# A state-space block on one Trainium2 core: channel chunks in interleaved pairs, tiles in pieces of two chunks, column-grouped sums

## The chip, the cores and the metric

The kernel runs on one core of one Trainium2 chip. A core has five instruction queues that run side by side: TensorE (PE in the profile: matmuls, results into PSUM), VectorE (DVE), ScalarE (ACT), GpSimd (POOL) and SyncE (SP, which here issues nearly all DMA transfers). The metric is the time of one execution on the device in microseconds, the median of several runs. The profile shows one more execution, with every instruction's start and end.

## What is computed

The input x is 8 images of 384 channels by 1024 positions, all in float32. Each image goes through a Mamba-like block and then (all but three of them) through a binarised MLP:

```python
t = layernorm(x over channels)                          # twice normed in the reference
xm, z = split(t @ in_proj_w.T)                          # 768 channels each
xc = silu(conv_w[0]*xm[l-2] + conv_w[1]*xm[l-1] + conv_w[2]*xm[l] + conv_b)
dt, Bm, Cm = split(xc @ x_proj_w.T, [24, 24 + 16])
dt = softplus(dt @ dt_proj_w.T + dt_proj_b)
for n in range(16):                                     # states, for each of 768 channels
    h[n][l] = exp(dt[l] * A[n]) * h[n][l-1] + dt[l] * xc[l] * Bm[l, n]
    y[l] += h[n][l] * Cm[l, n]
y = (y + xc * D) * silu(z)
x = x + gelu((y @ out_proj_w.T) @ mlp_w1.T + b1) @ mlp_w2.T + b2
```

The second layer works on the result: `x + bitlinear(gelu(bitlinear(layernorm(x), W1, b1)), W2, b2)`. A bitlinear takes the sign of W less its mean, in five groups of output rows, multiplies, and scales and clips the result by the largest absolute value over one image. Its groups cover five of the eight images; for the others this layer adds nothing.

## The kernel before

**Units of work.** Channels lie on the 128 partitions, positions along the free dimension, in two halves of T = 512. For image b:

- `s1(b)`, the front: norm, `in_proj` (p_in, p_z), the convolution, SiLU, `x_proj` (p_dbc), the rows of B and C (p_bc), `dt_proj` (p_dt), softplus, and the product dt times xc. The results xc, z, dt, dtx (dt times xc) and the B and C rows go to DRAM.
- `s2(b)`, the state space: `scan` takes 64 channels at a time (12 units an image). A tile has 32 channels times 4 states on its partitions, and 1024 positions. There are 8 tiles a unit: two groups of channels times four quads of states. For each tile ScalarE makes da = exp(A dt), GpSimd multiplies dtx by the row of B (L886, the B product) into u, VectorE runs the recurrence (L890), and the product with C follows, on GpSimd (L904) or VectorE (L907), as `on_pool` (L866) says. TensorE adds up the states through the small matrix `fold` into py (L842), 32 output rows a matmul, so that four matmuls share the array. Then y is gated with z and goes to DRAM as yg. Images 0 and 7 go through in halves, with the state carried between them; there one tile holds two groups of 32 channels by 512 positions.
- `s3(b)`: out_proj (p_out), the MLP (p_h, p_o), and the residual.
- `ffn(b)` for the first five images: the second layer. `binarise` (once for each of W1 and W2) adds up W with a matrix of ones (p_sums, L1018), takes the means (L1030), and writes the signs to DRAM.

**Order.** `write_down` lists all operations with what each reads and writes. `Plan.run` then sets the order on each queue ahead of time: it simulates the five queues with the costs given to `add`, and takes at each step an operation whose inputs and buffers are ready, by priority (sums of py first, then the scan of the current image, then fronts of the next two images, then `s3` and `ffn`). On the chip each queue runs in that fixed order and waits on semaphores. Where the plan leaves TensorE without work for more than 0.7 us it puts in stand-in matmuls (`spare`, L412), whose result nobody reads.

**Buffers.** Each tile belongs to a ring of a fixed number of buffers (L369 to L386), and a buffer comes free when its last reader is done. Those that the change touches: `front` (2 of six chunks: xc, dt, z), `dt_r` and `dtx_r` (3 each of 1024), `u` (9 tiles of 1024), `da` (2, in PSUM), `yg` (1 of six chunks), `hid` (2 of six chunks), `res` (2), `small` (7), and `sq` (1, the squares of the norm). A chunk is 128 channels by 512 positions.

**Helpers.** `load` (L462), `store` (L469) and `weights` (L484) issue one DMA on SP; `matmuls` (L489) issues n matmuls that add up in one PSUM bank; `act` (L506) is one ScalarE function; `affine` (L516) goes to ScalarE or, if it is free sooner, to VectorE or GpSimd.

Of the kernel before, what the change touches and what calls it, by code (L numbers as in the profile page):

```python
# [42 lines left out]
HK = KH // 2  # L43
T = 512
# [49 lines left out]

def c_pool(n):
    return 0.18 + n * 0.00214
# [33 lines left out]
class Piece:  # L130
# [8 lines left out]

    def __getitem__(self, part):  # L140
        return self, part

# [209 lines left out]
class Layer:  # L352
    def __init__(self, ctx, tc, a, out):
# [9 lines left out]
        def ring(tag, bufs, where=sbuf):  # L363
# [7 lines left out]
            "front": ring("front", 2), "t_f": ring("t_f", 2), "w_f": ring("w_f", 3),  # L371
            "dbc": ring("dbc", 1), "halo": ring("halo", 2),

            "dt_r": ring("dt_r", 3), "dtx_r": ring("dtx_r", 3), "u": ring("u", 9),
# [4 lines left out]
            "yg": ring("yg", 1), "hid": ring("hid", 2), "t_b": ring("t_b", 1), "w_b": ring("w_b", 3),  # L379
            "w6": ring("w6", 2), "w6_n": ring("w6_n", 2), "res": ring("res", 2),  # L380

            "t_n": ring("t_n", 2), "small": ring("small", 7),
# [9 lines left out]
        for b in range(B):  # L392
            for name in ("dt", "dtx"):
                self.dram[name, b] = handed(f"{name}_d{b}", [DI, L])
# [24 lines left out]

    def constants(self):
# [13 lines left out]
        self.pick = const.tile([P, 2 * NS], F32, name="pick")  # L436
        nc.vector.tensor_add(self.pick, ident[:, DQ : 2 * DQ], ident[:, DP + DQ : DP + 2 * DQ])
        self.edge = const.tile([P, KD, 2], F32, name="edge")
# [50 lines left out]
    def matmuls(self, p, w, t, k0, n, start, stop, r, claim, w0=0):  # L489


        def emit():
            for k in range(n):
                self.nc.tensor.matmul(  # L494
                    p.real, w.real[:, w0 + k, :], t.real[:, k0 + k, :],
                    start=start and k == 0, stop=stop and k == n - 1,
                )
# [100 lines left out]
    def s1(self, b):  # L598
# [6 lines left out]
        def by_pair(name, half, t):  # L605
            d = self.dram[name, b]
            self.store(d.real[:, half].rearrange("k p l -> p k l"), t, lambda x: x, [d[half]],
                       4 * P * KD * T)

        def tiled(name, half, t):  # L610
            d = self.dram[name, b]
            to = d.real[:, HALVES[half]].rearrange("(k p) l -> p k l", p=P)
            self.store(to, t, lambda x: x, [d[half]], 4 * P * KD * T)
# [14 lines left out]
        def gate(half, t):  # L628
            z = self.piece(r_z, [P, KD, T], "z")
            for m in range(KD):  # L630
                w = self.weights(r_w, KC, a["in_proj_w"][KD + m])
                pm = self.mm3(w, t, [t[k] for k in range(KC)], [z], "p_z")
                self.affine(
                    lambda m=m, z=z: z.real[:, m, :], lambda pm=pm: pm.real, [pm], [z[m]]
                )
            all_z = [z[m] for m in range(KD)]
            self.act(lambda z=z: z.real, lambda z=z: z.real, AF.Silu, c_act(KD * T),
# [634 lines left out]
```

## Time and profile before

| | |
|---|---|
| median of 3 runs | 3261.88 us (3261.76 to 3268.25) |
| the profiled execution | 3262.23 us |
| its span | 3260.4 us |
| TensorE busy | 3122.5 us (96%) |
| of it stand-ins, L412 | 80.0 us |
| GpSimd busy | 2848.7 us (87%) |
| VectorE busy | 2742.3 us (84%) |
| ScalarE busy | 2024.3 us (62%) |
| mean granted TensorE clock | 0.984 |
| DMA | 748.73 MB, mean 230 GB/s |

Times in the profile are microseconds from the span's start. A group of instructions shows its line, engine and operation, the output and input by the program's names, the shapes, the count (x), then busy time, the mean of one in ns, and after the second bar the idle time of its engine just before such instructions and what ended it. A float32 matmul leaves two records on TensorE, so counts of matmuls there are twice those in the code. Overlapping matmuls are counted once in the busy time. In a table of stretches each engine has its busy time and, in brackets, its number of instructions; the last columns are the granted clock, the busy share of the DMA engines and GB/s. A line of waits names the engine and its line, whom it waited for, the sum in us, how often, and the longest.

### The profile page before, as it was taken

How to read it: one execution, taken by the hardware profiler on the slowest of the kernel's cores; microseconds unless marked ns; L12 is line 12 of the kernel's file. 1: busy time of each engine (PE TensorE's matmuls, PEld its weight loads, DVE VectorE, ACT ScalarE, POOL GpSimd, SP SyncE). 2: the span in 40 equal slices, each digit the busy share in tenths (PEclk: the TensorE clock that was granted, in tenths of full speed). 3: DMA queues.
4: the chain of work that ended last, by engine and by line, in shares of the span. 5: the costliest groups of instructions: out<-in, count | busy, mean ns of one | idle time of the engine just before them, and what ended most of it. 6: DMA issues, size and time to landing. Idle time of an engine off the chain costs nothing.

```text
span 3260.4 us, 34027 instructions
## 1 busy us (share of the span) xinstructions
PE 3122.5 (96%) x11098; PEld 1317.7 (40%) x11098; DVE 2742.3 (84%) x2127; ACT 2024.3 (62%) x2246; POOL 2848.7 (87%) x1371
## 2 busy tenths in 40 slices
PE   8988999999999999999899999999999999999999
PEld 4333433444433434334334344343443534433334
DVE  4778899799978899888998878999788988789880
ACT  4778787656665576665656566755666565656551
POOL 1688899979999989999989999989999899999970
PEclk9998999999999999999999999999999999999999
DMA  6988778657796568675686667866677656766542
GB/s 218 305 282 276 249 250 294 221 183 234 259 322 197 184 230 291 229 238 197 208 298 211 237 211 246 295 225 226 220 275 250 207 185 205 249 187 207 167 141 76
DMA packets 367345, 748.73 MB, mean 230 GB/s; under 512 B 33856, under 2 KB 111168, under 8 KB 367168
## 3 DMA queue, kind: packets, MB, share of 16 engines
q1 hardware_dynamic: 366736, 746.46, 68.5%
q8 instruction: 89, 1.46, 0.2%
q14 instruction: 88, 0.72, 0.1%
q10 hardware_dynamic: 432, 0.09, 0.0%
HBM read 566.06 MB, written 180.36 MB: 229 GB/s over the span
## 4 chain that ended last, share of the span: by engine, by line
PE 74%; DMA 9%; DVE 6%; ACT 5%; issue 2%; POOL 2%; SPq 1%; ACTq 0%; DVEq 0%; POOLq 0%
PE p_y L494 17%; PE p_o L494 14%; PE p_h L494 13%; PE py L842 9%; PE p_out L494 6%; PE p_z L494 6%; PE p_in L494 5%; DVE da L890 2%; DMA w<-in_out_proj_w 2%; DMA w_f<-in_in_proj_w 2%; DVE u L890 1%; ACT L510 1%; DMA w_b<-in_mlp_w 1%; ACT da L510 1%; PE spare L412 1%
## 5 line engine op out<-in xcount | busy, mean ns | idle before, releaser
L886 POOL TENSOR_TENSOR u<-dtx_r,bc 128x1024 f32<-128x1024 f32 x768 | 1790.4, 2362 | 72.3 <-DMA dtx_r<-dtx_d 46.3
L510 ACT ACTIVATE da<-dt_r,a_neg 128x1024 f32<-128x1024 f32 (+1 forms) x960 | 902.7, 945 | 534.0 <-DVE u L907 331.1
L904 POOL TENSOR_TENSOR u<-u,bc 128x1024 f32<-128x1024 f32 x352 | 828.4, 2364 | 121.5 <-DVE u L890 115.5
L890 DVE TENSOR_TENSOR_SCAN da<-da,u 128x1024 f32<-128x1024 f32 (+1 forms) x416 | 840.5, 2020 | 111.6 <-POOL u L886 62.9
L890 DVE TENSOR_TENSOR_SCAN u<-da,u 128x1024 f32<-128x1024 f32 (+1 forms) x352 | 699.5, 2010 | 90.3 <-ACT da L510 63.0
L494 PE MATMUL p_h<-t,w_b 128*128 128x512 f32 x1152 | 513.6, 600 | 10.9 <-DMA w_b<-in_mlp_w 9.9
L907 DVE TENSOR_TENSOR u<-da,bc 128x1024 f32<-128x1024 f32 x416 | 507.9, 1221 | 10.5 <-ACT state L901 0.3
L494 PE MATMUL p_o<-g,w 128*128 128x512 f32 x1152 | 506.7, 595 | 5.4 <-ACT g L510 2.9
L842 PE MATMUL py<-u,fold 128*32 128x512 f32 x3072 | 376.6, 605 | 4.5 <-DVE u L907 4.5
L494 PEld LDWEIGHTS p_h<-t,w_b 128*128 128x128 f32 x1152 | 214.7, 190 | 298.1 <-issue 256.4
L494 PEld LDWEIGHTS p_o<-g,w 128*128 128x128 f32 x1152 | 215.9, 190 | 292.0 <-issue 277.3
L494 PE MATMUL p_y<-tn,w_b 128*128 128x512 f32 x720 | 324.9, 598 | 4.0 <-DVE tn L592 3.3
L494 PE MATMUL p_y<-gf,w_n 128*128 128x512 f32 x720 | 319.0, 599 | 6.7 <-DMA w_n<-bin_w 4.0
L510 ACT ACT_TABLE_LOAD x222 | 284.8, 1283 | 11.7 <-DVE xc L661 7.3
L494 PE MATMUL p_out<-yg,w 128*128 128x512 f32 x552 | 249.2, 604 | 8.9 <-DMA w<-in_out_proj_w 4.3
L494 PE MATMUL p_z<-t,w_f 128*128 128x512 f32 x504 | 232.5, 611 | 8.2 <-DMA w_f<-in_in_proj_w 6.2
L494 PE MATMUL p_in<-t,w_f 128*128 128x512 f32 x504 | 228.3, 602 | 10.8 <-DMA w_f<-in_in_proj_w 8.6
L494 PEld LDWEIGHTS p_y<-gf,w_n 128*128 128x128 f32 x720 | 135.1, 191 | 187.6 <-issue 172.4
L494 PEld LDWEIGHTS p_y<-tn,w_b 128*128 128x128 f32 x720 | 133.9, 190 | 183.9 <-issue 155.4
L842 PEld LDWEIGHTS py<-u,fold 128*32 128x32 f32 x3072 | 81.5, 110 | 261.1 <-issue 203.2
L525 ACT ACTIVATE g<-p_h,v_vecs 128x512 f32<-128x512 f32 x157 | 106.3, 681 | 120.9 <-PE p_h L494 120.7
L525 ACT ACTIVATE y<-p_y,v_vecs 128x512 f32<-128x512 f32 x138 | 94.1, 683 | 130.0 <-PE p_y L494 100.3
(112 smaller groups left out, 2700.3 us busy)
## 6 DMA issues: line engine op xcount, KB each, us to landing
dtx_r<-dtx_d SPq DMA_DIRECT2D x144, 512.0 KB, 5.8
dt_r<-dt_d SPq DMA_DIRECT2D x144, 512.0 KB, 6.0
w_b<-in_mlp_w SPq DMA_DIRECT2D x192, 192.0 KB, 2.9
w<-in_mlp_w SPq DMA_DIRECT2D x96, 384.0 KB, 3.6
w_f<-in_in_proj_w SPq DMA_DIRECT2D x168, 192.0 KB, 4.2
y_d<-y SPq DMA_DIRECT2D x120, 256.0 KB, 3.4
gf<-y_d SPq DMA_DIRECT2D x20, 1536.0 KB, 9.5
xc_d<-xc SPq DMA_DIRECT2D x16, 1536.0 KB, 7.3
```

The costliest lines, as they stand in the source:

```text
L412: self.plan.fill = lambda: self.nc.tensor.matmul(self.plan.spare.real[:, : 2 * P], self.ones, self.one.to_broadcast([P, 2 * P]), start=Tru ...
L494: self.nc.tensor.matmul(p.real, w.real[:, w0 + k, :], t.real[:, k0 + k, :], start=start and k == 0, stop=stop and k == n - 1,)
L510: lambda: self.nc.scalar.activation(out(), in_(), func, **{k: v() if callable(v) else v for k, v in kw.items()}),
L525: nc.scalar.activation(out(), in_(), AF.Identity, bias=bias, scale=scale)
L842: nc.tensor.matmul(py.real[p0 : p0 + DQ, :], self.fold, hc, start=False, stop=(q == NQUAD - 1), skip_group_check=True,)
L886: add("POOL", 2.36, lambda: nc.gpsimd.tensor_mul(u.real, dtx_r.real, spread(bq)), r=[dtx_r, bq], w=[u])
L890: add("DVE", (0.2 if half else 0.15) + n * 0.00209, lambda k=k, col=col: nc.vector.tensor_tensor_scan(to.real[:, k, :], da.real[:, k, :], ...
L904: add("POOL", 2.36, lambda: nc.gpsimd.tensor_mul(u.real, u.real, spread(cq)), r=[cq], w=[u])
L907: add("DVE", 1.21, lambda: nc.vector.tensor_mul(u.real, da.real, spread(cq)), r=[da, cq], w=[u])
```

## The change

**The state space in pairs.** A unit is still 64 channels, but they come from two chunks (2p and 2p+1), every fourth channel of each, in place of every second one of a chunk. The dtx of the two chunks is stored interleaved, position by position (`[KC, P, 2L]`), and so is u: `[128, 1, 1024, 2]`. One GpSimd instruction makes the B product of both groups, 2048 elements, with the row of B repeated for the innermost two; the C product is done in the same way where it is on GpSimd. The scans, the C products on VectorE and the py matmuls read and write every second element. For the last quad, u is the dtx tile itself. C products on GpSimd are now those of quads 0 and 2, and of quad 1 in every fourth unit.

```diff
-            "dt_r": ring("dt_r", 3), "dtx_r": ring("dtx_r", 3), "u": ring("u", 9),
+            "dt_r": ring("dt_r", 3), "dtx_r": ring("dtx_r", 2), "u": ring("u", 3),
...
+            dtxs = self.piece("dtx_r", [P, wide, n, 2], "dtx_r")
...
+                src = d.real[p, r0 + x :: G, at : at + 2 * n].unsqueeze(1)
...
+                u = dtxs if q == NQUAD - 1 else self.piece("u", [P, wide, n, 2], "u")
+                self.scan_pair(
+                    u, [[(k * G + g) * NQUAD + q for k, g in groups] for groups in tiles],
+                    n, dts, dtxs, b_q[q], c_q[q], state, half, self.on_pool(q, m),
+                )
...
+                        parts = [u.real[:, 0, h, i] for i in both for h in HALVES] if (
+                            half is None) else [u.real[:, x, :, i] for i in both for x in both]
...
-    def on_pool(self, i, q, m):
-
-        return q == 0 or (q == 2 and (i == 0 or m % 3))
+    def on_pool(self, q, m):
+
+        return q % 2 == 0 or (q == 1 and m % 4 == 0)
...
+        def product(t, x, row):
+            nc.gpsimd.tensor_mul(
+                u.real[:, x], t.real[:, x], row.real.unsqueeze(2).to_broadcast([P, n, 2])
             )
...
+        for x in range(wide):
+            add("POOL", c_pair(2 * n), lambda x=x: product(dtxs, x, bq), r=[dtxs[x], bq],
+                w=parts[x])
+        for t, mine in enumerate(cols):
+            da = self.piece("da", [P, wide, n], "da")
...
+            def in_u(i, t=t):
+                return u.real[:, 0, :, t] if wide == 1 else u.real[:, t, :, i]
...
+                    da=da, in_u=in_u: nc.vector.tensor_tensor_scan(
+                        to(i), da.real[:, i, :], in_u(i),
...
+                    if wide == 1:
+                        nc.vector.tensor_mul(u.real[:, 0, :, t], da.real[:, 0, :], cq.real)
...
         if on_pool:
-            add("POOL", 2.36, lambda: nc.gpsimd.tensor_mul(u.real, u.real, spread(cq)),
-                r=[cq], w=[u])
...
+            for x in range(wide):
+                add("POOL", c_pair(2 * n), lambda x=x: product(u, x, cq), r=[cq], w=parts[x])
```

**Pieces of two chunks.** A new class `Split` stands for a tile of several chunks and holds one ring buffer for every two. The tiles xc, z, dt, yg and g are split in that way; their in-place functions, loads and stores go piece by piece. The functions of one tile still wait, in the first piece, for all chunks (of `g`, for six). `mlp_out` adds up two chunks at a time.

```diff
-            "front": ring("front", 2), "t_f": ring("t_f", 2), "w_f": ring("w_f", 3),
+            "front": ring("front", 7), "t_f": ring("t_f", 2), "w_f": ring("w_f", 3),
...
-            "yg": ring("yg", 1), "hid": ring("hid", 2), "t_b": ring("t_b", 1), "w_b": ring("w_b", 3),
-            "w6": ring("w6", 2), "w6_n": ring("w6_n", 2), "res": ring("res", 2),
-
-            "t_n": ring("t_n", 2), "small": ring("small", 7),
+            "yg": ring("yg", 3), "hid": ring("hid", 6), "t_b": ring("t_b", 1), "w_b": ring("w_b", 3),
+            "w6": ring("w6", 2), "w6_n": ring("w6_n", 2), "res": ring("res", 4),
+
+            "t_n": ring("t_n", 2), "small": ring("small", 5),
...
+class Split:
...
+    def __init__(self, make, n, per):
+        self.pieces, self.per = [make() for _ in range(n // per)], per
...
+    def at(self, k):
+        return self.pieces[k // self.per].real[:, k % self.per, :]
...
+        def in_place(t, func, table):
+            parts = [t[k] for k in range(KD)]
+            for p, piece in enumerate(t.pieces):
+                mine = parts[p * PER : (p + 1) * PER]
+                self.act(lambda piece=piece: piece.real, lambda piece=piece: piece.real, func,
+                         c_act(PER * T), r=parts if p == 0 else mine, w=mine, table=table)
...
+            for k in range(0, HK, PER):
+                need = [g[i * HK + k + j] for j in range(PER)]
+                self.matmuls(po, w, g, i * HK + k, PER, i + k == 0, i * HK + k + PER == KH, need,
+                             claim, k)
```

**The dt rows on two row groups.** The x_proj result still comes in two halves of the sum. One full matmul with a constant `join` (p_all) adds them, and its copy puts the dt rows on partitions 0 to 31 and again on 32 to 63, B and C on 64 to 95. Then p_dt goes two chunks at a time, each with K = 32 on its own row group. The rows go to DRAM with one DMA in place of four. The product dtx is made pair by pair, and stored pair by pair.

```diff
-            def both_halves(dbc=dbc, p_bc=p_bc):
-                for g in range(G):
-                    nc.tensor.matmul(
-                        p_bc.real[g * DQ : (g + 1) * DQ, :], self.pick,
-                        dbc.real[:, g * TG : (g + 1) * TG], start=True, stop=True,
-                    )
...
+            add("PE", MM, lambda dbc=dbc, p_all=p_all: nc.tensor.matmul(
+                p_all.real[:n_all, :], self.join, dbc.real, start=True, stop=True
+            ), r=[dbc], w=[p_all])
...
+                    for i in range(2):
+                        rows = slice(i * DQ, (i + 1) * DQ)
+                        nc.tensor.matmul(
+                            pds[i].real, ws[i].real[rows, (k + i) % KC, :], dbc.real[rows, :],
+                            start=True, stop=True,
+                        )
...
+            for p in range(KC):
+                dtx = self.piece("sq", [P, T, 2], "dtx")
+                add("POOL", 2.35, lambda p=p, dtx=dtx, xc=xc, dt=dt: nc.gpsimd.tensor_mul(
+                    dtx.real.rearrange("p n i -> p i n"), xc.pieces[p].real, dt.pieces[p].real
+                ), r=[xc[2 * p], xc[2 * p + 1], dt[2 * p], dt[2 * p + 1]], w=[dtx])
```

The convolution's edge at the second half's start is worked out once in three small GpSimd instructions, and added piece by piece in three more.

**Sums for the binarisation.** The chunks of W go to three (W1) or four (W2) column groups of the array, 32 output rows each; VectorE adds up the groups of rows from PSUM, and a small matmul joins the column groups.

```diff
+        lanes = min(kt, G)
...
                 for k in range(ks.start, ks.stop):
+                    g = k % lanes
                     nc.tensor.matmul(
-                        pm.real, self.ones, w.real[:, k - ks.start, :],
-                        start=(k == 0), stop=(k == kt - 1),
+                        pm.real[g * DQ : (g + 1) * DQ, :], self.ones[:, :DQ],
+                        w.real[:, k - ks.start, :], start=(k < lanes), stop=(k >= kt - lanes),
                     )
```

The host lays out D, A_log and the last image's out_proj weights for the new order of channels.

## The prediction

> **What bounds the kernel now.** I read the busy times of the page first, then four stretches of the span, then the stand-in matmuls that the planner puts into gaps of TensorE, then the groups, and last who waited for whom.
>
> ```profile
> PE 3122.5 (96%) x11098; PEld 1317.7 (40%) x11098; DVE 2742.3 (84%) x2127; ACT 2024.3 (62%) x2246; POOL 2848.7 (87%) x1371
> ...
> PE 74%; DMA 9%; DVE 6%; ACT 5%; issue 2%; POOL 2%; SPq 1%; ACTq 0%; DVEq 0%; POOLq 0%
> ```
> TensorE is busy for 3122.5 of 3260.4 us and carries 74% of the chain that ended last. But GpSimd and VectorE are close behind, so the stages decide.
>
> ```profile
> core 0: us, PE busy (x) PEld busy (x) DVE busy (x) ACT busy (x) POOL busy (x), PEclk, DMA share, GB/s
> 0.00:116.00 116.00, 101.77 (x474) 51.00 (x475) 52.15 (x70) 59.90 (x74) 23.38 (x26) 0.97 0.77 258
> 116.00:400.00 284.00, 254.03 (x970) 106.77 (x968) 243.41 (x237) 221.10 (x299) 244.64 (x154) 0.95 0.82 267
> 400.00:3170.00 2770.00, 2680.25 (x9447) 1122.37 (x9444) 2438.45 (x1813) 1727.14 (x1858) 2580.73 (x1193) 0.99 0.69 230
> 3170.00:3261.00 91.00, 86.50 (x214) 37.57 (x212) 8.32 (x10) 16.12 (x17) 0.00 (x0) 0.99 0.25 75
> ```
> The first 116 us are the serial start, the last 91 us TensorE's alone. In the long stretch TensorE is idle for 2770 - 2680.25 = 89.8 us, GpSimd is busy for 93.2% and VectorE for 88.0%: three engines are nearly level.
>
> ```profile
> 400.00:3170.00 2770.00, 62.04 (x250) 46.36 (x250) 0.99 0.69 230
> ```
> This is the same stretch with the stand-ins (L412) alone: 62.0 us of TensorE's busy time there is filler. So 89.8 + 62.0 = 151.8 us of the stretch are gaps in which TensorE had nothing to do; useful is 2618.2 us. Over the whole span filler is 80.0 us, useful work 3042.5.
>
> ```profile
> L886 POOL TENSOR_TENSOR u<-dtx_r,bc 128x1024 f32<-128x1024 f32 x768 | 1790.4, 2362 | 72.3 <-DMA dtx_r<-dtx_d 46.3
> L904 POOL TENSOR_TENSOR u<-u,bc 128x1024 f32<-128x1024 f32 x352 | 828.4, 2364 | 121.5 <-DVE u L890 115.5
> L907 DVE TENSOR_TENSOR u<-da,bc 128x1024 f32<-128x1024 f32 x416 | 507.9, 1221 | 10.5 <-ACT state L901 0.3
> L842 PE MATMUL py<-u,fold 128*32 128x512 f32 x3072 | 376.6, 605 | 4.5 <-DVE u L907 4.5
> ```
> GpSimd is almost nothing but state-space products: 1790.4 + 828.4 = 2618.8 of its 2848.7 us. The L842 row shows four 32-column matmuls at once: 3072 records are 1536 matmuls (each f32 matmul leaves two), 384 sets of four, 0.98 us a set.
>
> ```profile
> L722 PE MATMUL p_dt<-dbc,w_f 128*128 128x512 f32 x168 | 81.9, 620 | 9.5 <-ACT dt L525 6.0 <-ACT rows L523 3.4
> L722 PE MATMUL p_dt<-dbc,w_b 128*128 128x512 f32 x24 | 11.4, 608 | 0.9 <-DVE xc L661 0.9
> L1018 PE MATMUL p_sums<-w,small 128*128 128x384 f32 x24 | 10.2, 578 | 3.3 <-DMA w<-in_W 3.3
> L1018 PE MATMUL p_sums<-w,small 128*128 128x512 f32 x18 | 8.5, 606 | 3.1 <-DMA w<-in_W 3.1
> L703 PE MATMUL p_bc<-dbc,pick 128*32 128x128 f32 x128 | 6.7, 281 | 2.0 <-ACT dbc L523 2.0
> ```
> These are the matmuls that the change replaces, shapes kept apart: (81.9 + 11.4)/96 = 0.97 us for one dt matmul.
>
> ```profile
> POOL u L904 <- DVE u L890: 115.5, 70, 10.6
> ...
> POOL u L886 <- PE py L842: 21.6, 11, 5.3
> ```
> Of GpSimd's waits, the C product waiting for VectorE's scan is the longest; lack of a free u costs 21.6 us.
>
> [...] 1024 elements take 2362 ns (L886), 512 take 1275 ns (L732), so 2.125 ns an element and 186 ns fixed. [...]
>
> **The change part by part.**
>
> TensorE. (1) dt: 96 matmuls become 48 sets of two on row groups. As one set of column groups costs 0.98 us I take 1.02 with the switch: 93.3 - 49 = 44 us less; if rows do not overlap, 0. (2) Binarisation: 9 + 12 matmuls (8.5 + 10.2 = 18.7 us) become 3 + 3 sets at 0.98, and two small mean matmuls at 0.3: 18.7 - 6.5 = 12 less. (3) p_bc (6.7 us) becomes 16 full p_all at 0.9: 8 more. (4) The py matmuls read u at a step of two floats; [...] the worst case is a doubling, 377 us. Sum: 48 us less, 4 if the rows do not overlap.
>
> GpSimd. B products stay 768 x 1024 elements. C products were 3.67 tiles of 8 per unit of 64 channels; `on_pool` now gives 4.5 (4.67 in the halved images): 436 tiles of 1024 in place of 352. Together 1.233 million elements in 754 instructions (480 B, 274 C), 140 us of fixed cost. What an element costs with B or C repeated innermost for two outputs the trace does not show. Above, 2.125 ns stays. Below, one-input clips (L1088: 3072 elements 2898 ns, L1160: 1536 take 1474) give 0.93, so the second input adds 1.2; if each fetch of it serves two outputs, 1.53. I take the middle, 1.83: 2256 + 140 = 2396 us, 223 less than 2619. At 2.125 it is 2760, 141 more. Level is (2619 - 140)/1233 = 2.01 ns. [...] The other GpSimd edits (pair dtx product 48 x 2.35 against 118.6, edge in four adds, clips in thirds) come to within 5 us.
>
> VectorE loses 84 products at 1.22: 103 us less. Its scans (2.28 us) and products now read or write u with a step of two[...]. If a strided write doubled the product, 332 x 1.07 = 355 us more.
>
> ScalarE: 100 whole-tile functions of 3072 become 300 of 1024. From 2765 and 1476 ns the fixed part is 0.19: 200 x 0.19 = 38 us more, hidden by the 38% in which ScalarE is idle; without that cover the exps would be late, and VectorE after them.
>
> SP: whole stores and loads become thirds (xc, z, dt, dtx +128, yg +28, gf +40), rows go from 64 to 16, dtx loads from 240 to 120; dt weights +16, and in the halved images (0 and 7) four row groups in place of two for xr, zr, yg: +120. Net 164 issues of some 0.45 us, 74 us spread over a queue that mostly waits for buffers; it holds up weights queued behind, and the cover is the two spare buffers of `w_b` and `w_f`. At the start SP is on the path: its issues stand one after another in the chain at 59 to 71 us. Against that, the first dtx store was issued at 82.7 though its product ended at 74.5, the first dtx load at 91.8, and the first B product came at 105.1; storing by pairs can bring that forward by up to 10. I take the start at zero, plus or minus 15.
>
> Waits. In s1 the row of dbc, copy, p_all, copy, dt adds one matmul and one copy (0.9 + 0.58) to each front; fronts run ahead of the scan by two, so other matmuls hide it, except at the first, where 1.5 us is paid. u goes from 9 tiles to 3 pairs, the last quad writing over its own dtx: 6 + 2 tiles in place of 9. The next unit's third B product then waits for the last py of this unit, and behind it on GpSimd stand the C products and so VectorE's next scans. Bound: nothing, or the 21.6 us of that wait doubled, which the freed 223 us cover.
>
> Where the gain ends up. TensorE's 48 us come off the bound. Of the 151.8 us of gaps some are DMA waits, some are there because the scan, held by GpSimd at 93%, gives no new yg; GpSimd falls to about 85% of the stretch and VectorE to 84%, and I take a quarter to go: 151.8/4 = 38, less 5 for the start's serial copy and SP's issues. Sum 48 + 33 = 81. The profiled execution took 3262.23 us (span 3260.4 and 1.8 around it), 0.35 above the median of 3261.88: 3262 - 81 = **3181 us**.
>
> **The rivals.**
> - Only the matmuls count (3215 to 3255, about 3235). Gaps do not shrink, because they are DMA waits and shallower buffers bring new ones: 3262 - 48 + 21 for the u wait doubled. For it: chain 9% DMA, stretch 116 to 400 at 82% DMA share. Against it: filler clusters late (2500 to 2800 us), where DMA is at 0.56 to 0.66.
> - Slower: GpSimd becomes the bound. Place: `product`, price 2.125 ns an element. GpSimd then has 2849 + 141 = 2990 us, of which some 2967 fall between 116 us and the tail; at 95%, as in many stretches of 100 us (93 on the mean), 3123, plus 116 and 91: about 3330; at 97%, 3266. It decides from about 2.05 ns up, just above the level 2.01. [...]
> - Strided access is not free (VectorE's product or py doubled): 355 us on an engine with 330 idle in the stretch, or 377 on TensorE: 3350 to 3600.
> - The row groups do not overlap: 44 us of the forecast are missing, 3225. That is the first rival's place.
>
> **How the numbers follow.** Likeliest case (3110 to 3215): 0.58. Only matmuls, rows not overlapping included: 0.17. GpSimd bound: 0.16. Strides dear: 0.05. Nothing to be told, within 0.2% or 6.5 us: 0.04; about that is what a measurement of this kernel tells from no change. Faster is 0.58 + 0.17 = 0.75, same 0.04, slower 0.21. The gaps could close by two thirds (100 us: 3114), so the low end is 3110; the high end, 3275, takes in the first rival, no change and the cheap end of the GpSimd case, and leaves out some 0.18 above. The likeliest case's own range is 3110 to 3215.
>
> **What would show it.** Right: the pair product of 2048 elements takes near 186 + 2048 x 1.83 = 3930 ns (4540 means the slower rival); scans stay at 2.28 and strided products at 1.22; p_dt falls to about 49 us, p_sums to 6; filler and idle of TensorE together fall by some 33 us; GpSimd's waits for py stay under 45. Wrong: py above 0.98 us a set, a B product waiting long for py, or a first B product later than 105 us.

## The result

| | before | after |
|---|---|---|
| median | 3264.64 us (4 runs, 3261.76 to 3268.25) | 3282.62 us (4 runs, 3280.4 to 3288.55) |
| ratio, 95% interval | | 1.0052 (1.0032 to 1.0071) |
| span of the profiled execution | 3260.4 us | 3282.3 us |
| TensorE: useful + stand-ins + idle | 3042.5 + 80.0 + 137.9 | 3057.6 + 50.7 + 174.0 |
| GpSimd / VectorE / ScalarE busy | 2848.7 / 2742.3 / 2024.3 | 2727.3 / 2665.0 / 2028.2 |

Useful is TensorE's busy time less the stand-ins. The changed kernel takes 18 us more, where 81 less were forecast. GpSimd and VectorE did become lighter. TensorE, which carries the end, did not: it works 15 us more on its own sums, and its gaps (stand-ins and idle) grew from 217.9 to 224.7 us. The page of after, busy times and the shares of the chain that ended last:

```profile
PE 3108.3 (95%) x10874; PEld 1274.0 (39%) x10874; DVE 2665.0 (81%) x2081; ACT 2028.2 (62%) x2402; POOL 2727.3 (83%) x1029
...
PE 70%; DMA 12%; DVE 7%; ACT 4%; POOL 3%; issue 2%; SPq 1%; ACTq 0%; DVEq 0%; POOLq 0%
```

TensorE still leads the chain; 3 points more of it are DMA. The same four stretches of after, all engines, then the third one for the stand-ins alone:

```profile
0.00:116.00 116.00, 96.55 (x433) 46.75 (x434) 53.91 (x85) 60.57 (x77) 31.48 (x32) 0.91 0.81 272
116.00:400.00 284.00, 244.74 (x940) 97.53 (x941) 240.86 (x236) 221.47 (x322) 243.53 (x156) 0.89 0.78 256
400.00:3170.00 2770.00, 2658.32 (x9224) 1083.58 (x9217) 2339.23 (x1733) 1718.93 (x1969) 2433.67 (x835) 0.98 0.70 231
3170.00:3283.00 113.00, 108.64 (x288) 46.15 (x286) 31.01 (x29) 27.23 (x37) 18.58 (x9) 0.99 0.27 81
```

```profile
400.00:3170.00 2770.00, 33.77 (x132) 23.90 (x132) 0.98 0.70 231
```

In the long stretch GpSimd fell from 93.2% to 87.9% and VectorE from 88.0% to 84.4%, where 85 and 84 were forecast. The gaps there are 2770 - 2658.32 + 33.77 = 145.5 us, 6 less than before's 151.8 and not 38 less. The first 400 us lost 14 us of TensorE's busy time, and their clock is 0.91 and 0.89 where it was 0.97 and 0.95: (1 - clock) times the time is 42 us, against 18. In the trace the granted clock has two levels, whole and half, and the half-clock stretches last 3.4, 6.8 or 10.2 us (one 13.7; the last one of each trace is cut short by the end of the span): 108.8 us in all before, 169.9 after. In each trace all of them begin on one grid of 3.413 us. Of the grid's windows at whole clock, those with 2 us or more of idle time on TensorE were all followed by half clock (17 of 17 before, 20 of 20 after), those with less than 1 us almost never (none of 878, 3 of 863).

Where TensorE's 15 us come from, by tile in the two traces: p_dt 93.4 to 68.2, p_sums 18.7 to 6.9, p_bc's 6.7 to 17.6 of p_all and 0.9 of p_means, py 376.6 to 386.9: together -14.9. The sums that the change does not touch took 30 us more (p_z +13.4, p_y +7.0, p_o +4.6, p_in +3.2, the others less). Half clock accounts for the first two: p_z ran 39.6 us of its time at half clock where it was 17.3 before, p_y 22.9 where it was 3.9, and half of these 41 us is 21 (one p_z matmul starts 1.707 us after another at half clock and 0.858 us at whole clock, medians of after). It does not account for the other two: p_o meets no half-clock stretch in either trace and p_in as much as before (10.2 and 9.8 us); their 8 us stay open. Half clock also weighs on the dt pairs, 19.6 of p_dt's 68.2 us against 3.4 of 93.4 before.

The groups of after, shapes kept apart (columns as before):

```profile
L914 POOL TENSOR_TENSOR u<-dtx_r,bc 128x2048 f32<-128x2048 f32 x216 | 881.4, 4092 | 183.2 <-issue 93.8 <-PE py L879 78.8 <-DMA dtx_d<-dtx 7.2
L939 DVE TENSOR_TENSOR_SCAN u<-da,u 128x1024 f32<-128x1024 f32 x324 | 738.6, 2283 | 113.3 <-POOL u L914 66.9 <-ACT da L538 36.3 <-ACT t L551 1.7
L914 POOL TENSOR_TENSOR u<-u,bc 128x2048 f32<-128x2048 f32 x162 | 662.2, 4090 | 49.2 <-DVE u L939 44.9 <-issue 2.2 <-DMA w_n<-bin_w 1.9
L959 DVE TENSOR_TENSOR dtx_r<-da,bc 128x1024 f32<-128x1024 f32 x144 | 176.3, 1224 | 3.8
L755 PE MATMUL p_dt<-dbc,w_f 32*128 32x512 f32 x168 | 57.5, 699 | 8.0 <-DMA w_f<-in_dt_proj_w 3.5 <-ACT dt L553 2.3 <-ACT dbc L551 2.1
L734 PE MATMUL p_all<-dbc,join 128*96 128x512 f32 x32 | 17.6, 634 | 1.7 <-ACT dbc L551 1.7
L1094 PE MATMUL p_sums<-w,small 128*32 128x512 f32 x18 | 4.0, 752 | 4.2 <-DMA w<-in_W 4.1
L1094 PE MATMUL p_sums<-w,small 128*32 128x384 f32 x24 | 2.9, 563 | 2.6 <-DMA w<-in_W 2.6
```

The pair product takes 4092 ns for 2048 elements, and in the halved images 2137 for 1024: 1.91 an element and 0.18 us fixed. The strided scan (2283, before 2278) and the strided C product (1224, before 1221) cost what they did. The first row's idle column is new: 78.8 us waiting for py, and 93.8 shown as "issue". These are waits for py too: in 23 of the 25 cases the product begins 0.16 to 0.17 us after a group of py matmuls has ended. The sums of waits of GpSimd, TensorE and SP's queue in after:

```profile
POOL u L914 <- issue: 98.5, 25, 12.0
POOL u L914 <- DVE u L939: 94.7, 55, 8.8
POOL u L914 <- PE py L879: 83.6, 34, 9.7
```

```profile
PE p_z L522 <- DMA w_f<-in_in_proj_w: 27.8, 13, 7.0
PE p_h L522 <- DMA w_b<-in_mlp_w: 20.8, 14, 3.6
```

```profile
SPq L808 <- PE py L879: 167.4, 81, 6.9
SPq L836 <- DMA yg_d<-zr: 113.5, 66, 4.7
SPq L899 <- DVE zr L895: 44.2, 30, 4.9
```

Two rows of SP's waits in before, for the same loads of dtx_r and the same stores of yg:

```profile
SPq L863 <- DVE zr L859: 161.0, 68, 9.8
SPq L771 <- POOL u L886: 128.1, 93, 7.1
```

The wait for a free u went from 21.6 to some 180 us. On SP the loads of dtx_r (L808) now wait for py's last matmul, 81 times, since the dtx tile is the last quad's u. Before, they waited for GpSimd's B product, and SP's waits for py were 5.8 us. SP does not wait longer as a whole (the sum of its waits is 2175 us before and 2163 after): the store of yg, which comes after py, waits less. What is new is which issues stand behind the wait for py. Weights come late: p_z waited 6.2 us for w_f before, p_h 9.9 for w_b; all TensorE idle time that ended with a DMA rose from 55.8 to 95.6 us.

### The profile page after: what moved, and what is told of

The parts are those of the page before. It is cut to its first block, busy times and chain, and to the rows that moved or that the text cites. A ratio compares the mean times of both kernels' runs of the same rounds, so it can differ in the third digit from the quotient of the medians.

```text
span 3282.3 us, 33586 instructions
## 1 busy us (share of the span) xinstructions
PE 3108.3 (95%) x10874; PEld 1274.0 (39%) x10874; DVE 2665.0 (81%) x2081; ACT 2028.2 (62%) x2402; POOL 2727.3 (83%) x1029
## 4 chain that ended last, share of the span: by engine, by line
PE 70%; DMA 12%; DVE 7%; ACT 4%; POOL 3%; issue 2%; SPq 1%; ACTq 0%; DVEq 0%; POOLq 0%
PE p_y L522 16%; PE p_o L522 13%; PE p_h L522 12%; PE py L879 9%; PE p_out L522 6%; PE p_z L522 5%; PE p_in L522 4%; DMA w_f<-in_in_proj_w 3%; POOL u L914 2%; DVE u L939 2%; DVE da L939 2%; DMA w_b<-in_mlp_w 2%; DMA dtx_r<-dtx_d 1%; ACT da L538 1%; PE p_dt L755 1%
## 5 line engine op out<-in xcount | busy, mean ns | idle before, releaser
L914 POOL TENSOR_TENSOR u<-dtx_r,bc 128x2048 f32<-128x2048 f32 (+1 forms) x360 | 1186.1, 3310 | 196.1 <-issue 93.8
L914 POOL TENSOR_TENSOR u<-u,bc 128x2048 f32<-128x2048 f32 (+1 forms) x274 | 901.3, 3293 | 102.3 <-DVE u L939 92.2
L939 DVE TENSOR_TENSOR_SCAN u<-da,u 128x1024 f32<-128x1024 f32 (+1 forms) x436 | 868.1, 2006 | 142.4 <-POOL u L914 91.5
L939 DVE TENSOR_TENSOR_SCAN da<-da,dtx_r 128x1024 f32<-128x1024 f32 (+1 forms) x192 | 388.0, 2021 | 74.7 <-POOL dtx_r L914 43.5
L914 POOL TENSOR_TENSOR dtx_r<-dtx_r,bc 128x2048 f32<-128x2048 f32 (+1 forms) x120 | 396.6, 3310 | 0.9
L522 PE MATMUL p_y<-gf,w_n 128*128 128x512 f32 x720 | 326.0, 607 | 12.0 <-ACT gf L538 6.2
L939 DVE TENSOR_TENSOR_SCAN da<-da,u 128x1024 f32<-128x1024 f32 (+1 forms) x140 | 286.0, 2043 | 19.3 <-ACT da L538 10.3
L879 PE MATMUL py<-u,fold 128*32 128x512 f32 x2304 | 300.5, 623 | 0.0
L522 PE MATMUL p_z<-t,w_f 128*128 128x512 f32 x504 | 245.8, 637 | 33.9 <-DMA w_f<-in_in_proj_w 27.8
L522 PE MATMUL p_in<-t,w_f 128*128 128x512 f32 x504 | 233.2, 610 | 18.7 <-DMA w_f<-in_in_proj_w 12.4
L553 ACT ACTIVATE g<-p_h,v_vecs 128x512 f32<-128x512 f32 x160 | 109.0, 684 | 165.3 <-PE p_h L522 164.9
L959 DVE TENSOR_TENSOR dtx_r<-da,bc 128x1024 f32<-128x1024 f32 x144 | 176.3, 1224 | 3.8
```

What stands on the lines that cost most here:

```text
L522: self.nc.tensor.matmul(p.real, w.real[:, w0 + k, :], t.at(k0 + k), start=start and k == 0, stop=stop and k == n - 1,)
L553: nc.scalar.activation(out(), in_(), AF.Identity, bias=bias, scale=scale)
L879: nc.tensor.matmul(py.real[g * DQ : (g + 1) * DQ, :], self.fold, hc, start=False, stop=(q == NQUAD - 1), skip_group_check=True,)
L914: nc.gpsimd.tensor_mul(u.real[:, x], t.real[:, x], row.real.unsqueeze(2).to_broadcast([P, n, 2]))
L939: da=da, in_u=in_u: nc.vector.tensor_tensor_scan(to(i), da.real[:, i, :], in_u(i), state.real[:, col : col + 1] if half else 0.0, ALU.mult ...
L959: nc.vector.tensor_mul(u.real[:, 0, :, t], da.real[:, 0, :], cq.real)
```

## The experiments

There are two kinds. Where an edit changes what the planner sees (a cost, a ring, an operation fewer), the written order changes throughout. Where only the emitted instruction's shape changes, the order is kept. Ratios are to runs of the kernel before that were taken together with the experiment's, so experiments are compared by their ratios and not by their medians. The last three columns are TensorE's times in the profiled execution, in us.

| run | median, us | ratio (95%) | useful | stand-ins | idle |
|---|---|---|---|---|---|
| e1_order_before | 3268.40 | 1.0006 (0.9993 to 1.0020) | 3040.6 | 84.3 | 145.3 |
| e2_order_after | 3303.11 | 1.0100 (1.0066 to 1.0135) | 3061.1 | 64.8 | 174.7 |
| e3_relief_before | 3314.22 | 1.0149 (1.0121 to 1.0178) | 3047.0 | 100.1 | 161.8 |
| e4_less_pe_before | 3279.00 | 1.0042 (1.0029 to 1.0054) | 3016.0 | 76.0 | 184.4 |
| e5_cost_after | 3324.77 | 1.0182 (1.0157 to 1.0206) | 3056.7 | 80.7 | 188.6 |
| e6_weights5_after | 3275.82 | 1.0038 (1.0024 to 1.0051) | 3032.3 | 80.4 | 164.9 |
| e7_no_inplace_after | 3297.11 | 1.0103 (1.0083 to 1.0124) | 3042.7 | 93.6 | 157.4 |
| e8_weights5_cost_after | 3302.21 | 1.0120 (1.0099 to 1.0142) | 3055.7 | 73.9 | 176.7 |
| e15_weights5_drain_after | 3263.38 | 0.9996 (0.9989 to 1.0003) | 3041.5 | 69.0 | 147.7 |
| e16_weights4_before | 3263.19 | 0.9996 (0.9988 to 1.0003) | 3029.5 | 83.8 | 137.1 |
| **order kept:** e9_stride_before | 3272.00 | 1.0029 (1.0013 to 1.0045) | 3053.1 | 80.0 | 132.2 |
| e10_contig_after | 3270.58 | 1.0023 (1.0009 to 1.0037) | 3038.3 | 51.1 | 175.5 |
| e11_relief_kept | 3252.73 | 0.9974 (0.9963 to 0.9984) | 3039.8 | 79.8 | 130.4 |
| e12_dt_kept | 3264.52 | 1.0003 (0.9990 to 1.0017) | 3018.8 | 80.4 | 164.9 |
| e13_ph_kept | 3247.61 | 0.9949 (0.9937 to 0.9961) | 3016.4 | 79.2 | 150.2 |
| e14_mm_kept | 3208.23 | 0.9829 (0.9816 to 0.9842) | 2908.3 | 79.3 | 223.2 |
| e17_relief_dt_kept | 3249.38 | 0.9956 (0.9941 to 0.9971) | 3021.0 | 79.3 | 153.1 |
| e18_relief_mm_kept | 3168.95 | 0.9705 (0.9687 to 0.9722) | 2895.7 | 80.0 | 195.9 |

**How much is the order alone?** One constant of the planner, the same in both kernels:

```diff
-LOAD_TABLE = 1.29
+LOAD_TABLE = 1.31
```

> The kernel before with one constant of the planner changed: the cost that it reckons for a load of a function table, 1.29 to 1.31 us. No instruction is added, removed or altered; only the order on the queues differs. Theory 1, the order alone moves the time by as much as the whole change did: the time differs from the kernel before by 0.3% or more, 10 to 30 us, either way. Theory 2, the change's 18 us are the cost of its own parts and the order is neutral: within 5 us of the kernel before.

> The changed kernel with the same constant at 1.31: the same instructions in another order. Theory 1: it differs from the changed kernel's 3282 us by 10 us or more. Theory 2: within 5 us of it.

The kernel before does not move; the changed one moves by some 16 us (1.0100 against 1.0052; the intervals just touch), with the same work apart from stand-ins. So a few tenths of a per cent between versions planned anew can come from the written order alone.

**The two reliefs, planned anew.** Left out are the C products of quads 1 and 2 of the first group (e3), and every second dt matmul (e4):

```diff
+        if i == 0 and q in (1, 2):
+            return 2
...
+        skip = on_pool == 2
...
+        if skip:
+            return
         if on_pool:
             add("POOL", 2.36, lambda: nc.gpsimd.tensor_mul(u.real, u.real, spread(cq)),
```

```diff
+                if k % 2 == 0:
+                    pd = self.piece("mm", [P, T], "p_dt")
...
```

> The kernel before, leaving out the product with C for two of the eight tiles of each unit (first group, quads 1 and 2), so that the output lacks that factor there: GpSimd loses 96 products (227 us), VectorE 96 (117 us), about what the forecast took the change to free. The forecast's step, gaps of TensorE close when GpSimd is relieved: 38 us or more less, 3224 or below. Rival, TensorE's own work and its late weights set the end: no less than 3250, and up to 3290 if the order falls badly.

> The kernel before, leaving out every second dt matmul (48 of 96; the odd chunk takes the even one's result, so the output is another): 46 us of TensorE gone. If TensorE's work is passed on to the end: 3215 to 3225. If the gaps take it up (other waits end later in its place, as in the changed kernel): 3245 or more.

Both came out slower with less to do. In e3 the scan ended at 3056 us where it had ended at 3179, and this stretch followed (columns as in the stretches above):

```profile
3058.00:3312.00 254.00, 246.94 (x579) 109.61 (x577) 10.52 (x14) 45.80 (x49) 0.00 (x0) 0.99 0.28 87
```

After 3058 us TensorE works on with the scan over (GpSimd 0.00), busy for 246.9 of the 251 us to the end of the span at 3308.9. The planner had put the scan first and left TensorE's other work for the end, and the gaps earlier (161.8 + 100.1 us over the span) were not used for it. A relief of the scan is worth nothing here unless TensorE's total (useful and gaps) falls. e4 has 27 us less work than before and 42 us more of gaps. Neither separates the work from the order, so both were repeated with the order kept.

**The same reliefs, order kept.** e11 makes those C products on an eighth of their positions, e12 makes each dt matmul on half of its positions (the copy repeats them), e17 does both:

```diff
+        short = n // 8 if on_pool in (2, 3) else n
...
-            add("DVE", 1.21, lambda: nc.vector.tensor_mul(u.real, da.real, spread(cq)),
+            add("DVE", 1.21, lambda: nc.vector.tensor_mul(
+                u.real[:, :, :short], da.real[:, :, :short], spread(cq)[:, :, :short]),
```

```diff
-                    pd.real, w.real[:, k % KC, :], dbc.real, start=True, stop=True,
+                    pd.real[:, : T // 2], w.real[:, k % KC, :], dbc.real[:, : T // 2],
+                    start=True, stop=True,
```

> The kernel before with its order kept; the product with C of the first group is made on an eighth of the positions in quads 1 and 2 (the rest lacks that factor): about 183 us less on GpSimd and 88 on VectorE, with every instruction in its place. The forecast's step, gaps close when GpSimd is relieved: 30 us less or more, 3235 or below. Rival, TensorE sets the end: within 10 us of the kernel before. If this is level while the third run was 48 us slower, the third run's loss was the order's.

> The kernel before with its order kept; each dt matmul makes 256 of its 512 positions, and the copy repeats them (another output): some 43 us less on TensorE in the same places where the change saves. If TensorE's work is passed on: 3215 to 3230. If waits close by (the copies of p_dt, weights) take its place: 3245 or more. The fourth run, 46 us less and slower, is then the order's in the first case.

> The kernel before in its own order, with both reliefs that the prediction counted on at once: the dt matmuls take half of the positions (the other half copies the first), 34 us less of TensorE, and the C products of quads 1 and 2 of the first group take an eighth of theirs, some 240 us less of GpSimd and 87 us less of VectorE. The prediction's sum would say 34 + 38 = 72 us faster, ratio 0.978. If the two do not help each other, it is what they gave apart, 0 and 8.5 us: ratio 0.997. If each was held back by the other, it is 20 us or more, ratio below 0.994.

240 us less on GpSimd and 87 on VectorE are worth 8.5 us. The dt matmuls, from e12's groups:

```profile
L722 PE MATMUL p_dt<-dbc,w_f 128*128 128x256 f32 x168 | 52.7, 440 | 17.3 <-ACT dt L525 12.4 <-ACT rows L523 4.9
L722 PE MATMUL p_dt<-dbc,w_b 128*128 128x256 f32 x24 | 6.9, 405 | 1.8 <-ACT dt L525 0.9 <-DVE xc L661 0.9
```

93.4 became 59.6 us, and the time stayed where it was. Of the 34 us, TensorE's useful time shows 24: the other sums took 10 more (p_out 6 of them, with 12 us more of it at half clock; the half-clock stretches rose from 108.8 to 150.0 us). And its idle time rose by 27 us: 16 more of it ended by ScalarE, 6 by DMA, 5 by VectorE. Only 9 of the 27 stand right before the dt matmuls, in most part waits for ScalarE's copies of earlier dt sums (6.0 us before, 12.4 here, in the first row). Both at once gave 14.4 us (e17), where the prediction's own terms for such a relief are 34 + 38 = 72. That is a little more than the 0 and 8.5 of the parts; the intervals do not tell much more.

**Is TensorE the bound at all?** e13 shortens the second and third matmul of each p_h to 460 of 512 positions, e14 (without the condition on the name) all but the first matmul of each call of `matmuls`; e18 is e14 with e11. In all three the last 52 positions lack terms.

```diff
+                m = 460 if k and p.name == "p_h" else T
                 self.nc.tensor.matmul(
-                    p.real, w.real[:, w0 + k, :], t.real[:, k0 + k, :],
+                    p.real[:, :m], w.real[:, w0 + k, :], t.real[:, k0 + k, :m],
```

> The kernel before in its own order; only the second and third matmul of every p_h (the MLP's first layer, three matmuls after one another) take 460 of the 512 positions, so that hidden sums of the last 52 positions lack two thirds. TensorE then has 384 matmuls less by a tenth of 0.89 us, 34 us less work, the size of what the halved dt matmuls took away to no effect. Theory A, TensorE's own work in dense streaks sets the end and only savings between waits are lost: 20 to 34 us faster, ratio 0.990 to 0.994. Theory B, the waits for other queues set the end everywhere and TensorE's savings turn into idle time: ratio 0.998 to 1.001, gaps up by some 30 us.

> The kernel before in its own order; all matmuls of the fronts' and both MLPs' sums but the first of each group take 460 of the 512 positions, so that the last 52 positions lack terms. TensorE has about 165 us less work, all five times the step of the p_h run. Theory A: 100 to 165 us faster, ratio 0.95 to 0.97. Theory B: at most 30 us faster, ratio 0.99 to 1.0, filler unchanged (its number is fixed by the order) and idle time up by more than 130 us, since the scan on GpSimd and VectorE then sets the end. In between, the scan takes over after some 50 us: ratio about 0.98.

> The kernel before in its own order, with the shortened sums (134 us less of TensorE's useful work in the run that had them alone, 55 us faster) and the shortened C products (240 us less of GpSimd, 87 less of VectorE, 8.5 us faster alone). If TensorE and the scan hold the end together, so that each relief waits for the other, the two give well over 64 us, 90 to 130: ratio 0.960 to 0.972. If they add, 64 us: ratio 0.980. If something third holds (the DMA queue and the weights), no more than the 55 us: ratio 0.983.

TensorE's useful work fell by 26.1, 134.2 and 146.8 us; by the ratios the end moved by 16.6, 55.8 and 96 us. So a saving does pass, about 0.6 of a small one in dense sums and 0.4 of a large one; theory A's size was too high, theory B is excluded, and e14 came out at the middle case that its expectation named. The chain of e14, then of e18:

```profile
PE 35%; DVE 19%; POOL 16%; DMA 14%; ACT 8%; issue 6%; SPq 1%; DVEq 0%; ACTq 0%; POOLq 0%
```

```profile
PE 48%; DMA 15%; DVE 12%; POOL 10%; ACT 9%; issue 5%; SPq 2%; DVEq 0%; POOLq 0%; ACTq 0%
```

In e14 TensorE's share of the chain has fallen from 74% to 35% and the scan's engines have risen from 8% to 35%: the scan takes over. Lighten it now (e18) and another 40 us come (0.9829 to 0.9705), where the same relief gave 8.5 us while TensorE was full: 96 together, and 64 as the sum of the parts. The two hold the end together, and each pays only as far as the other has room.

**What does py's step of two cost?** e9 lets before's py read u at a step of two, e10 lets after's read it without one; both then add up other positions than the reference does, with the order kept.

```diff
-                            (h * DP + i * DQ, hc.real[:, 0, HALVES[h]])
+                            (h * DP + i * DQ, hc.real[:, 0, h::2])
...
```

> The kernel before with its order kept; only the py matmuls read u at a step of two floats (every second position, so the output is another). In the changed kernel a group of 16 py records takes 2.006 us, before 1.924, 15.7 us over 192 groups. If the step makes them dearer: 2.00 us or more here, and up to 16 us more time, 3266 to 3282. If the 0.08 us come from something else in the changed kernel (the order, the clock): 1.93 us and no change.

> The changed kernel with its order kept; the py matmuls read 512 contiguous floats of the pair tile (which mixes the two groups, so the output is another). If the step is dear: the group of 16 falls to about 1.93 us and the time by up to 16 us, 3266 to 3282. If not: 2.006 stays, time within 5 us of the changed kernel.

The rows of py in e9 (before has 376.6 and 605 in this row), then those of after and of e10:

```profile
L842 PE MATMUL py<-u,fold 128*32 128x512 f32 x3072 | 391.5, 623 | 4.4 <-DVE u L907 4.4
```

```profile
L879 PE MATMUL py<-u,fold 128*32 128x512 f32 x2304 | 300.5, 623 | 0.0
L879 PE MATMUL py<-dtx_r,fold 128*32 128x512 f32 x768 | 103.7, 611 | 0.0
```

```profile
L879 PE MATMUL py<-u,fold 128*32 128x512 f32 x2304 | 289.5, 605 | 0.0
L879 PE MATMUL py<-dtx_r,fold 128*32 128x512 f32 x768 | 100.8, 597 | 0.0
```

The two rows of after, and those of e10, overlap in time, so they do not add up. The median group of eight py matmuls (two sets of four) takes 1.924 us without the step and 2.006 with it, in either kernel (2.007 in e9): 4%, or 192 x 0.082 = 15.7 us. It moves the end by 0.0029 of the time in both directions, 9.5 us (e9 up, e10 down from after's 1.0052); e9's interval leaves 4 to 15 us. Of the changed kernel's 18 us about half is this.

**The late weights and the u buffers.** e7 gives the last quad a u of its own (four pairs, paid for with `front` at 6 and `res` at 2):

```diff
-                u = dtxs if q == NQUAD - 1 else self.piece("u", [P, wide, n, 2], "u")
+                u = self.piece("u", [P, wide, n, 2], "u")
```

> The changed kernel with a u of its own for the last quad (four pairs of u) in place of the dtx tile, so that dtx is free after its last B product; the space comes from one piece of front and two of res. If the dtx tile held until the py sums blocks SP's queue and so delays the weights: SP's waits for py fall from 174 us to under 30, TensorE's waits for DMA from 96 to about 60, time 3262 or below. Rival: SP's waits for py go, TensorE's waits for DMA stay above 80, time 3270 to 3305.

The rows of SP's and GpSimd's waits in e7:

```profile
SPq L836 <- DMA yg_d<-zr: 45.2, 42, 3.2
SPq L493 <- PE py L879: 6.8, 10, 0.9
```

```profile
POOL u L914 <- PE py L879: 105.7, 43, 10.0
POOL u L914 <- issue: 72.6, 18, 16.6
```

The loads of dtx_r no longer wait for py (what is left, 6.8 us, is on other loads; before has 5.8), SP's wait for yg_d is back at before's 44.7, and TensorE's idle time ended by DMA fell from 95.6 to 53.7 us, below before's. In the changed kernel's three orders with three weight buffers and the dtx tile as u it is 87 to 103 us (after, e2, e5), so 53.7 is more than chance of order is seen to do. That the dtx_r load behind py made the weights late is therefore likely, but not shown with the order kept: e7 has an order and rings of its own, and SP's waits as a whole are as long as in after (2149 us). And the kernel is not faster: stand-ins rose from 50.7 to 93.6 us, and GpSimd still waits some 180 us for u. What the late weights cost is not shown.

e6 gives `w_f` and `w_b` five buffers in place of three (`front` 6, `res` 3; the first diff), e5 tells the planner the measured costs (a dt pair 1.42, in the second diff, and p_all 1.1), e8 does both, e15 is e6 with the planner's constant DRAIN at 0.25 in place of 0.2, and e16, with that constant too, gives the kernel before four buffers of each, at the price of one u tile:

```diff
-            "front": ring("front", 7), "t_f": ring("t_f", 2), "w_f": ring("w_f", 3),
+            "front": ring("front", 6), "t_f": ring("t_f", 2), "w_f": ring("w_f", 5),
...
-            "yg": ring("yg", 3), "hid": ring("hid", 6), "t_b": ring("t_b", 1), "w_b": ring("w_b", 3),
+            "yg": ring("yg", 3), "hid": ring("hid", 6), "t_b": ring("t_b", 1), "w_b": ring("w_b", 5),
```

```diff
-                add("PE", MM + 0.2, two, r=[dbc, *dict.fromkeys(ws)], w=pds, claim=[dt.pieces[k // PER]])
+                add("PE", 1.42, two, r=[dbc, *dict.fromkeys(ws)], w=pds, claim=[dt.pieces[k // PER]])
...
```

> The changed kernel with five buffers in place of three for the weights of s1 (w_f) and of the MLP (w_b); the space comes from one piece of front and one of res. Theory, late weights: TensorE's waits for DMA fall from 96 us to under 60, the stretches at half clock from 170 us to under 130, and the time to 3240 to 3262. Rival, the order decides: the waits go elsewhere and the time stays at 3270 to 3305.

> The changed kernel with two of the planner's costs set to what its trace shows: 1.42 us for two dt matmuls on row groups (planned 1.06) and 1.10 for p_all (planned 0.86). The work is the same. If these two wrong costs (21 us over the span) drive the queues out of step with the plan: 20 us or more less than the changed kernel, 3262 or below, with fewer waits of TensorE. If not: the change of order alone, 3270 to 3305.

> The fifth and sixth run's edits together: measured costs and five weight buffers. Theory, late weights and wrong costs each cost some 20 us: 3225 to 3250. Rival, order decides: 3265 to 3305, not the sum of the two.

> The kernel after with five weight buffers in each ring in place of three, as in the run before with five, and the planner's constant for TensorE's drain at 0.25 in place of 0.2, which gives the order with the earliest reckoned end of those reckoned (3162 in the plan's own terms, 3174 for after). If the plan's own end tells something of the chip, it is below 3265 us, ratio under 1.0; if the order is a matter of chance within some 30 us, it is between 3270 and 3305, ratio 1.002 to 1.012.

> The kernel before with eight tiles of u in place of nine and four weight buffers in each ring in place of three, planned with the drain constant at 0.25 (with 0.2 no order comes out with eight). If late weights are what its gaps are made of, TensorE's idle time ended by DMA falls from 56 to about 30 us and it takes some 25 us less, ratio 0.99; if the gaps only move, ratio 1.0 to 1.01.

Truer costs made it slower, by 42 us (e5 against after). Deeper weight rings lower TensorE's idle time ended by DMA (95.6 to 67.8 in e6, 33.9 in e8) and yet decide nothing: e8, with the least of it, is slower than after, and e16, with 47.6 against before's 55.8, is level with before. The best version of the changed kernel, e15, is level too (0.9996); its TensorE lay at half clock for 118.7 us, where it was 169.9 in after, and did 16 us less of useful work. The changed program in its several orders and rings spans 0.9996 to 1.0182, 60 us, with the same arithmetic. No version faster than before came out that computes the whole.

## Why the prediction was wrong

The forecast was 3181 us and faster; it is 3282.6 and slower. By its steps:

- **GpSimd's and VectorE's costs**: right in kind. The pair product was put at 1.83 ns an element, an estimate between 1.53 and 2.125, and takes 1.91; state-space products are 881.4 + 662.2 + 304.8 + 294.6 + 239.1 + 102.1 = 2484 us, 135 less and not 223. It is below the level of 2.01, so the rival in which GpSimd becomes the bound fell by its own criterion. VectorE became 77 us lighter and not 103, but its strides cost nothing (scan 2278 to 2283 ns, product 1221 to 1224), as the forecast had it. ScalarE took 4 us more and not 38.
- **dt on row groups, 93.3 to 49**: half right. In 33 of the 48 pairs the two matmuls start together and are done within 1.13 us, where the sum had 1.02; the others take 1.14 to 3.92, and the group is 68.2 us: 1.42 a pair on the mean, against 2 x 0.97 one after another. Of the eight pairs above 2 us seven ran mostly at half clock; in four pairs at whole clock the second matmul began 0.17 to 0.53 us after the first. The profile of before had only column groups side by side, so the 49 was the author's estimate. That two row groups overlap is now shown, and a mean gain of 1.37 for two (2 x 0.97 over 1.42) is what it was worth here.
- **p_bc to p_all, +8**: +10.9, at 1.10 each and not 0.9. **Binarisation, -12**: -11.8, right; the two mean matmuls are under 1 us.
- **py's step of two, put at no cost**: wrong, by 15.7 us of work and about 9.5 of time (e9, e10). The zero was the author's assumption; no view of before shows a read or write of u at this step. It held for VectorE (scan and product within 5 ns) and not for the operand that TensorE reads (u, in py: 1.924 to 2.006 us a group). The rival "strided access" named it, and its size (a doubling, 377 us) was 24 times too large.
- **"TensorE's 48 us come off the bound"**: the step that failed. The change's own edits save 14.9 us on TensorE, not 48: dt gave 25 of its 44, and py took 10 where nothing was put. The untouched sums took 30 more, a term that the sum did not have, two thirds of it in sums that lay longer at half clock. And the rate was wrong: 34 us off these dt matmuls, order kept, move the end by nothing (e12); they turned into slower sums and idle time elsewhere. In dense sums half or so passes (e13, e14).
- **"I take a quarter to go", 38 us of gaps**: the other step that failed. A relief larger than the change's gave 8.5 us (e11), and the gaps in the long stretch fell by 6. GpSimd at 93% was read as a scan that starves TensorE. While TensorE is full, the scan has slack; only where TensorE gave room first (e18 against e14) did it pay 40. The two terms were added as if each were the only bound.
- **The rival "only the matmuls count"** comes nearest in mechanism: the gaps did not close, and the wait for u and late weights came, as it said. It too kept the 48 us, and so ended on the wrong side.
- **Waits on u, "nothing, or 21.6 doubled"**: some 180 us on GpSimd. The bound was taken from a ring of nine single tiles, where the wait was rare; with three pairs GpSimd waits 59 times, with nine tiles 11 times. Here the prediction's own sign of being wrong came, a B product waiting long for py; so did py above 0.98 us a set (1.003). The 121 us by which GpSimd became lighter are less than this.
- **SP, +164 issues hidden**: the count was exact (2089 to 2253 issues). What was missed is what the prediction itself had to ask, who stands behind a waiting instruction: the dtx_r load that waits for py most likely held the weights (e7).
- **Start, 0 give or take 15**: the first B product came at 94.9 us, 10 earlier than before. The first unit was done 12 us earlier, and by unit 50 of 96 the lead was gone; the loss builds up after that, 26 us at the last unit. Half clock, which the sum had no term for, ate part of the start's gain: 82 us of it in the first 400 us, against 34.

What stays open: how much of the remaining half of the 18 us is late weights, how much half clock, and how much the chance of one written order. e2 and e5 show the last to be as large as the whole effect; e15 shows that the changed program need not be slower. None of them was taken out alone with the order kept. No run takes out the pieces of two chunks, or the smaller ring of `small`, either.

## What to carry to other kernels

When two chains are close to level, do not add a saving on one to a share of the gaps on the other: test each with the order of the instructions kept, by shortening an instruction in place, and then both at once. A kernel whose order is planned ahead of time has a spread of its own (here 60 us over orders and ring sizes with the same arithmetic), which has to be known before a change of less than that is read. And when a buffer's last reader moves to another engine (here dtx_r's, from GpSimd to TensorE), look at who fills it: its load now waits for another engine (the loads of dtx_r waited 167.4 us for py, where all of SP waited 5.8 us for py before), and everything behind it in its queue waits with it.

## What was not expected of the hardware

- Reading u at a step of two floats costs TensorE's float32 py matmuls 4% (1.924 to 2.006 us a group), while VectorE's scan (2278 to 2283 ns) and product (1221 to 1224 ns) at the same step cost nothing.
- A GpSimd product with one operand repeated for each two outputs takes 1.91 ns an element beyond a fixed 0.18 us (4092 ns for 2048, 2137 for 1024), where plain ones take 2.125 (2362 ns for 1024, 1275 for 512).
- Half-clock stretches begin on a grid of 3.413 us, and 2 us of idle time within one window of it were followed by half clock in all 37 cases of before and after. They took 3 to 6% of the span and grew where work was taken from TensorE with the order kept (108.8 us before, 150.0 in e12, 184.3 in e14).
